# Gate weights through a line in DRAM, and basis groups moved around the batch norms

## The chip, the cores and the metric

The kernel runs on one core of a Trainium2 chip. The metric is device microseconds (us) from start to end of one execution; 510.31 us is the median of 3 runs before the change (509.25 to 510.54).

The core has engines with instruction streams of their own: PE (matrix products; its weight loads are shown apart as PEld), DVE (elementwise work and reductions), ACT (elementwise functions), POOL (here mostly an issuer of transfers) and SP (here only an issuer of transfers). Data lies in SBUF (128 partitions), products come out in PSUM banks of 128 x 512 float32, and transfers between DRAM and SBUF are done by 16 DMA engines.

## The reference, cut to what matters

Four graph layers run over one graph of 512 nodes with 512 features. Each is `x = x + layer(relu(layernorm(x)))`: an attention layer (L0), a GIN of two rounds with batch norm (L1), a GCN (L2) and a gated relational layer of two rounds (L3). The change touches L1's second half, L2 and what L3 needs:

```
# L1, twice (l = 0, 1)
h = x + segment_sum(x[src], dst)
h = prelu(h @ conv_W1[l].T + conv_b1[l], conv_a[l]) @ conv_W2[l].T + conv_b2[l]
x = relu(batchnorm(h) * bn_gamma[l] + bn_beta[l])
# L2
out = leaky_relu(segment_sum((h @ W)[src] * norm, dst) + b)
# L3, twice: weights of each relation r from 30 bases
w[r]  = sum_b att[r, b] * basis[b]                 # basis: 30 x 512 x 512
gate  = sigmoid(x_j @ gate_w[r, :, 0])
msg_r = gate[:, None] * x_j @ w[r]
out   = segment_sum(msg of the edge's type, row) + x @ root + bias
```

## The kernel before

All edges are first counted into dense 512 x 512 matrices, so every segment sum is a product ("gather" below). A 512 x 512 array is held as 4 blocks of 128 partitions, T = 4; P = 128.

**Order of the work.** The source is a trace of instructions in program order. The tool that builds the kernel may let an instruction run earlier or later on its engine when its inputs are planned to be ready; an instruction wrapped in `on(...)` (or `keep_in_program_order`) stays behind the instruction that stands before it in the source on the same engine. An engine carries out its stream in the order so fixed, and waits where an input is late. The products of a gather stand in an `If` of PE alone (`exactly`), which picks one of two arithmetic forms.

**Two streams of bases.** L3's weighted sums over 60 bases of 1 MB are computed while the layers before run. The bases come over SP's queue into 4 buffers (`bases`, AHEAD = 4), in the order of the string `USES`: "P" is a group of 15 (or 7) bases' slices that PE multiplies by a small matrix of attention weights (one `basis_step`, 4 products with 32 output rows each, line 242), "V" is one whole basis that DVE adds into `wrel` in four steps (`advance(more)`, lines 266 to 274, tile `wrel` or `w`). The load of an entry of `USES` is issued when the entry four places before it has been used up, and SP issues in the order of the string. Two PE groups (round l = 0) or three (l = 1) fill one bank `bas`, of which there is only one. After the last of them ACT copies it to SBUF and stores it to DRAM (`leave`, lines 246 to 249); the next group can start only when the copy has read the bank. With `held`, the copy is not put in at once but noted, and put in where `leave()` is called (line 1067).

**The stretch of the change**, in the order of the source:

- Lines 967 to 1022, for l = 0 and 1: the gather into four banks `acc` (for l = 1 at line 976), `advance(more, 3)`, four copies into `aT` by DVE and ACT in turn (lines 978 to 983), then for l = 0 a `basis_step` and four DVE steps, for l = 1 two DVE steps; the first product with a bias and PReLU, two DVE steps after each block; the second product with the batch norm's statistics (`moments`, `normed`). `settle` flips a normalised block (four transposes on PE, line 337) and for l = 0 writes `xn`, which the next gather reads; for l = 1 adds it to `x`. Between the last blocks stand `basis_step(1)` and `basis_step(3 - l)`.
- Lines 1023 to 1027, after l = 1: eight products (two instructions each) for the two gate rows of L3's second round (`gate_rows(1)`: a gate column broadcast along the free axis times the identity, line 809, so that all 128 partitions hold the row), then one `basis_step` whose copy is held.
- Lines 1049 to 1066: L2's layer norm over four blocks, `moments`, `root` (ACT), `scale` (DVE), `normed_to` (ACT), all in `on`; a gather of blocks 0 and 1, then one of blocks 2 and 3. `xn` has two parts: ACT writes the rounded one, DVE the remainder (`F`).
- Lines 1067 to 1079: the held copy, ACT's copies of the gate rows of the second round into the tile `apart`, four copies into `aT`, and products and copies for the gate rows of the first round into two tiles of the pool `rows` (five buffers).
- Lines 1080 to 1091: L2's product, leaky ReLU, layer norm, and after the fourth block `basis_step(3)`, which uses up the last groups. (The `basis_step(1)` at line 1155 then finds none.)
- From line 1149: L3. `Layer.look` (line 1105, DVE) multiplies rows of `h` by a gate row and sums, `begin` (line 1111, PE) multiplies by the root weights, `messages` (line 324) and `end` (line 1145) follow.

Of the forty PE groups, counted from 0, those with number 16 + 3n, 17 + 3n and 18 + 3n belong together in round l = 1. Before the change the group at line 1027 is number 36, the third of its three.

Of the kernel before, what the change touches and what calls it, by code (L numbers as in the profile page):

```python
# [8 lines left out]
F32 = mybir.dt.float32  # L9
# [8 lines left out]
P = 128  # L18
N = 512
D = 512  # L20
T = N // P
# [9 lines left out]
RB = 4  # L31
STEPS = 2
BANKS = 8
USES = "P" * 26 + "VPVVVPPVVVPPPPVVVVPPPPPPPVVVVVVVVVVVV"
FEW = 4095
LESS = 2.0 ** -12
GW = 32
# [12 lines left out]
BQ, BK, B1, CB1, CB2, GAM, BET, GW1, GW2, NCOL = 0, 4, 8, 16, 24, 32, 40, 48, 56, 64  # L50
# [24 lines left out]
def gnn_kernel(ctx: ExitStack, tc: tile.TileContext, out: bass.AP, a: dict):  # L75
    nc = tc.nc
# [4 lines left out]
    rpool = ctx.enter_context(tc.tile_pool(name="rows", bufs=5))  # L81
# [17 lines left out]
    def ps():  # L99
        turn[1] += 1  # L100
        return bank(turn[0][turn[1] % len(turn[0])])
# [20 lines left out]
    ident = const.tile([P, P], F32, name="ident")  # L122
# [22 lines left out]
    cols = const.tile([P, NCOL], F32, name="cols")  # L145
# [8 lines left out]
    apart = const.tile([P, T, N], BF16, name="apart")  # L154
# [64 lines left out]
    dram = ctx.enter_context(tc.tile_pool(name="dram", bufs=1, space=bass.MemoryType.DRAM))  # L219
# [5 lines left out]
    def basis_step(n=1, keep=lambda ins: ins, held=None):  # L225
        for _ in range(n):
            if len(done) == len(loads):
                return
            l, n, g = loads[len(done)]
            done.append(n)  # L230
            assert USES[bases.at] == "P"
            t = bases.take()
            if g == 0:
                sums[:] = [pbas.tile([P, 512], F32, tag="bas", name="bas")]
            if g < STEPS:
                k, at = FULL * NQ, 32 - 2 * NQ * (g + 1)
                lhsT = wide[l][:k, at:at + 32]
            else:
                k = STEPS * HALF_OF * NQ
                lhsT = wide2[:k, :]  # L240
            for j in range(RB):
                tc.keep_in_program_order(nc.tensor.matmul(  # L242
                    sums[0][32 * j:32 * j + 32, :], lhsT=lhsT,
                    rhs=t[:k, j, :], start=(g == 0), stop=(g == STEPS + l - 1)))
            if g == STEPS + l - 1:
                def leave(n=n, bank=sums[0]):
                    o = spool.tile([P, 512], F32, tag="sums", name="sums")
                    keep(nc.scalar.copy(o, bank))  # L248
                    nc.scalar.dma_start(summed[l][n], o)

                if held is None:
                    leave()
                else:
                    held.append(leave)
# [9 lines left out]
    def accumulate(l, to):  # L264

        for b in range(ONPE[l], NB):
            assert USES[bases.at] == "V"
            t = bases.take()
            for r in range(2):
                at = AT1 + 2 * NB * l + NB * r + b  # L270
                for i in range(0, T, 2):
                    on(nc.vector.scalar_tensor_tensor(to[r][:, i:i + 2, :], t[:, i:i + 2, :], scal[:, at:at + 1],  # L272
                                                      to[r][:, i:i + 2, :], op0=ALU.mult, op1=ALU.add))
                    yield
# [51 lines left out]
    def ts(i):  # L326
        return slice(i * P, (i + 1) * P)

    def on(ins):

        return tc.keep_in_program_order(ins)
# [14 lines left out]
    def moments(mv, v, keep=lambda ins: ins):  # L346
        st = stat("st", 6)
        keep(nc.vector.bn_stats(st, v))
        keep(nc.vector.bn_aggr(mv, st))  # L349
# [42 lines left out]
    p = ps()  # L392
# [297 lines left out]
    def advance(gen, n=1):  # L690
        for _ in range(n):
            next(gen, None)
# [15 lines left out]
    plan, passes, at, halves = {}, 0, FIRST, 0  # L708
    waits = None
    for i, what in enumerate(line):  # L710
        at = max(at, FIRST + (len(order) - 2 - FIRST) * passes // whole)
        at = next((e for e in ends if abs(at - e) < 7), at)
# [87 lines left out]
    Cl = late.tile([P, T, N], F32, name="Cl")  # L800
    wrel = [wrel_load(0, r, late.tile([P, T, 512], F32, tag="wrel", name="wrel", bufs=2)) for r in range(2)]
    more = accumulate(0, wrel)
    def gate_rows(l, out):

        banks = [ps() for _ in range(2)]
        for r, p in enumerate(banks):
            for k in range(T):
                at = (GW1, GW2)[l] + 2 * k + r
                on(nc.tensor.matmul(p[:, ts(k)], lhsT=cols[:, at:at + 1].to_broadcast([P, P]), rhs=ident,
                                    start=True, stop=True))  # L810
        yield
        for r, p in enumerate(banks):
            on(nc.scalar.copy(out[r], p))
        yield out

# [149 lines left out]
    for l in range(2):  # L967

        aT = big("E")
        if l:  # L970
            acc = [bank("acc") for _ in range(T)]

            def emit(f, c):
                for m in range(T):
                    product(acc[m], [(f(xn[i][:, k, ts(m)]), Clx[c][:, k, :]) for k in range(T) for i in range(2)])
            exactly(emit)
            advance(more, 3)
        for m in range(T):
            p = acc[m]
            if m % 2:  # L980
                on(nc.vector.tensor_copy(aT[:, m, :], p))  # L981
            else:
                on(nc.scalar.copy(aT[:, m, :], p))
        if l == 0:
            basis_step(1, on)
            advance(more, 4)
        else:
            advance(more, 2)
        w = weights.take()
        h1T = big("B")  # L990
        for m in range(T):
            p = ps()
            product(p, [(w[:, k, ts(m)], aT[:, k, :]) for k in range(T)])
            at = CB1 + T * l + m
            z = small.tile([P, 512], F32, name="z")
            nc.scalar.activation(z, p, AF.Identity, bias=cols[:, at:at + 1])
            u = small.tile([P, 512], F32, name="u")
            nc.vector.tensor_scalar(u, z, 0.0, scal[:, CA + l:CA + l + 1], op0=ALU.min, op1=ALU.mult)
            nc.vector.scalar_tensor_tensor(h1T[:, m, :], z, 0.0, u, op0=ALU.max, op1=ALU.add)
            advance(more, 2)  # L1000
        w = weights.take()
        h2T = big("D")
        if l == 0:
            xn = parts("A", "G")
        for m in range(T):
            p = ps()
            product(p, [(w[:, k, ts(m)], h1T[:, k, :]) for k in range(T)])
            at = CB2 + T * l + m
            on(nc.scalar.activation(h2T[:, m, :], p, AF.Identity, bias=cols[:, at:at + 1]))
            if m:  # L1010
                normed(l, h2T, m - 1, moment)
            moment = stat("mv", 2)
            moments(moment, h2T[:, m, :])
            if m > 1:
                settle(l, h2T, m - 2, xn)
            if l and m < 3:
                advance(more)
        basis_step(1)
        normed(l, h2T, 3, moment)
        settle(l, h2T, 2, xn)  # L1020
        basis_step(3 - l)
        settle(l, h2T, 3, xn)
        if l:
            held = []
            gates = gate_rows(1, [apart.bitcast(F32).rearrange("p t n -> p (t n)")[:, N * r:N * r + N] for r in range(2)])
            next(gates)
            basis_step(1, on, held)

# [7 lines left out]
    def root(t):  # L1038
        on(nc.scalar.activation(sd4[:, t:t + 1], mv[:, t, 1:2], AF.Sqrt, bias=eps))
# [6 lines left out]
    def normed_to(to, t):  # L1046
        on(nc.scalar.activation(to[:, t, :], x[:, t, :], AF.Relu, bias=nm[:, t:t + 1], scale=by[:, t:t + 1]))

    for t in range(T):
        moments(mv[:, t, :], x[:, t, :], on)  # L1050
        root(t)
        if t:
            scale(t - 1)
        if t > 1:
            normed_to(xn[0], t - 2)
    scale(3)
    for t in (0, 1):
        normed_to(h, t)
# [7 lines left out]
    gather((2, 3), apart=True)  # L1066
    for leave in held:
        leave()
    second_w = next(gates)
    aT = big("E")  # L1070
    for m in range(T):
        if m % 2:
# [1 line left out]
        else:  # L1074
            on(nc.scalar.copy(aT[:, m, :], acc[m]))
    l2_b, bias2, bias = rows.take(), rows.take(), rows.take()
    gates = gate_rows(0, [rpool.tile([P, 512], F32, tag="row", name="row") for _ in range(2)])
    next(gates)
    first_w = next(gates)
    h = big("D")  # L1080
    for t in range(T):
        p = ps()
        product(p, [(aT[:, k, ts(t)], w[:, k, :]) for k in range(T)])
        z = small.tile([P, 512], F32, name="z")
        nc.vector.scalar_tensor_tensor(z, p, dinv[:, t:t + 1], l2_b, op0=ALU.mult, op1=ALU.add)
        u = small.tile([P, 512], F32, name="u")
        nc.vector.scalar_tensor_tensor(u, z, SLOPE, z, op0=ALU.mult, op1=ALU.max)
        nc.vector.tensor_add(x[:, t, :], x[:, t, :], u)
        norm_relu(h[:, t, :], x[:, t, :])
        if t == 3:  # L1090
            basis_step(3)

    class Layer:

# [144 lines left out]
```

## Time and profile before

| What | us |
|---|---|
| Median of 3 runs | 510.31 |
| The profiled execution's own time | 511.07 |
| Its span, first to last instruction | 509.1 |
| PE busy | 483.9 (95% of the span) |
| DVE busy | 399.3 (78%) |
| ACT busy | 195.6 (38%) |
| POOL busy | 37.9 (7%) |
| Gate products, line 809, 32 of 275 ns each | in four groups of 8, at 356.45 to 358.4 and 370.52 to 372.46 |
| ACT copies of gate rows, line 813 | 4 of 0.59 |
| One PE group, line 242 | 1.04 to 1.07 |
| One DVE step of a whole basis, line 272 | 1.25 to 1.28 |

How to read it: times inside the execution count from the start of the span. A line of the timeline gives start, duration, engine, line, operation, output and inputs, how many, and in brackets the idle time before it with what ended that. A line of the chain of waits gives start, duration and work of the chain that ended last. A line of the windows gives a stretch, its length, then busy us (and instructions) of PE, PEld, DVE, ACT and POOL, then the TensorE clock that was granted (1 is full), the DMA engines' busy share and GB/s.

### The profile page before, as it was taken

What the parts mean: (1) busy time and instruction counts of PE and PEld (TensorE: products, weight loads), DVE (VectorE), ACT (ScalarE), POOL (GpSimd) and SP (SyncE); (2) the same over time, 40 slices, a digit from 0 to 9 for tenths busy, and PEclk for the clock granted to TensorE, in tenths of its full rate; (3) what the DMA queues carried; (4) which work ended last, traced back from release to release, by engine and by line L of the source; (5) the groups of instructions that cost most, each with busy time, mean ns of one, the idle gap of its engine ahead of it and who ended that gap; (6) DMA issues with size and microseconds to landing.
All of it is one profiled execution on the core that took longest, in us unless ns stands there. A gap on an engine that the chain in (4) does not pass through costs nothing.

```text
span 509.1 us, 5732 instructions
## 1 busy us (share of the span) xinstructions
PE 483.9 (95%) x2014; PEld 249.0 (49%) x2014; DVE 399.3 (78%) x748; ACT 195.6 (38%) x318; POOL 37.9 (7%) x81
## 2 busy tenths in 40 slices
PE   3999999999999999999999999899899999999996
PEld 2333333255564547864445444444654584446642
DVE  6847487879999779999885974797659999998611
ACT  4876779724444213223332134115624610133000
POOL 7000000100000021310040000000010100000000
PEclk9999999999999999999999999999899999999999
DMA  8999768998968499586552695866944965420011
GB/s 243 282 248 250 180 175 194 230 258 198 216 160 198 105 226 293 220 227 191 210 182 84 149 238 195 305 184 156 269 143 154 287 190 217 165 82 3 0 42 41
DMA packets 42951, 94.06 MB, mean 185 GB/s; under 512 B 2113, under 2 KB 2567, under 8 KB 42919
## 3 DMA queue, kind: packets, MB, share of 16 engines
q1 hardware_dynamic: 34682, 68.17, 49.7%
q0 software_dynamic: 5712, 21.07, 13.9%
q10 hardware_dynamic: 2525, 4.39, 2.6%
q8 instruction: 20, 0.33, 0.3%
q14 instruction: 12, 0.10, 0.1%
HBM read 88.38 MB, written 5.24 MB: 184 GB/s over the span
## 4 chain that ended last, share of the span: by engine, by line
PE 67%; DVE 18%; ACT 8%; issue 2%; DMA 2%; ACTq 0%; DVEq 0%
PE pr L324 19%; PE acc L1145 11%; PE pg L324 10%; PE acc L1111 5%; PE ps L484 4%; PE acc L947 3%; PE bas L242 3%; DVE sc L648 3%; ACT sc L649 3%; ACT hs L553 3%; DVE sc L666 3%; PE ao L562 2%; DMA basis<-in_basis 2%; DVE half L642 2%; PE ps L497 2%
## 5 line engine op out<-in xcount | busy, mean ns | idle before, releaser
L272 DVE SCALAR_TENSOR_TENSOR wrel<-basis,scal,wrel 128x1024 f32<-128x1024 f32 x60 | 74.0, 1281 | 3.9 <-DMA basis<-in_basis 3.9
L553 ACT ACTIVATE hs<-iot,key 128x512 f16<-128x512 f16 x75 | 48.8, 711 | 5.5 <-PE ao L562 4.7
L549 DVE TENSOR_SCALAR hd<-iot,key 128x32 f16<-128x32 f16 (+1 forms) x132 | 33.3, 293 | 15.4 <-PE ao L562 15.2
L242 PE MATMUL bas<-basis,wide 120*32 120x512 f32 (+1 forms) x320 | 43.5, 600 | 0.7 <-ACT sums L248 0.7
L272 DVE SCALAR_TENSOR_TENSOR w<-basis,scal,w 128x1024 f32<-128x1024 f32 x32 | 39.3, 1276 | 0.0
L562 PE MATMUL ao<-hs,hd 128*32 128x512 f16 x204 | 25.8, 397 | 2.8 <-ACT hs L553 2.6
L649 ACT ACTIVATE sc<-sc 128x2048 f32<-128x2048 f32 (+1 forms) x10 | 15.7, 1568 | 32.6 <-DVE sc L648 32.6
L484 PE MATMUL ps<-bigB,w 128*128 128x512 f32 x56 | 27.2, 615 | 0.9 <-ACT bigD L487 0.6
L324 PE MATMUL pr<-bigE,w 128*128 128x512 f32 x48 | 21.6, 596 | 1.4 <-DVE bigE L981 1.4
L1195 DVE TENSOR_TENSOR u<-acc,x 128x512 f32<-128x512 f32 (+1 forms) x5 | 2.8, 582 | 23.5 <-PE acc L1145 23.5
L324 PE MATMUL pr<-bigD,w 128*128 128x256 f32 x88 | 20.2, 380 | 0.0
L555 DVE TENSOR_SCALAR hs<-iot,key 128x512 f16<-128x512 f16 x57 | 19.2, 345 | 0.0
L648 DVE TENSOR_TENSOR sc<-sc,half 128x2048 f32<-128x2048 f32 (+1 forms) x10 | 18.6, 1862 | 0.2
L666 DVE TENSOR_TENSOR sc<-sc,rec 128x2048 f32<-128x2048 f32 x8 | 18.3, 2284 | 0.0
L633 PE MATMUL psc<-bigC,bigD 64*128 64x256 f32 x128 | 18.2, 402 | 0.0
L324 PEld LDWEIGHTS pr<-bigD,w 128*128 128x128 f32 x88 | 16.6, 190 | 3.0 <-ACT bigE L891 0.8
L356 ACT ACTIVATE sd<-mv,eps 128x1 f32<-128x1 f32 x16 | 4.7, 296 | 34.4 <-DVE mv L349 33.4
L562 PEld LDWEIGHTS <-hd 128*32 128x32 f16 x204 | 6.1, 94 | 24.2 <-issue 15.4
L324 PE MATMUL pr<-w,bigE 128*128 128x512 f32 x40 | 17.8, 592 | 0.0
L484 PEld LDWEIGHTS ps<-bigB,w 128*128 128x128 f32 x56 | 9.7, 189 | 14.9 <-issue 11.1
L664 DVE RECIPROCAL rec<-ps 128x256 f32<-128x256 f32 x8 | 14.0, 1752 | 3.7 <-PE ps L660 3.7
L635 ACT COPY sc<-psc 128x1024 f32<-128x1024 f32 x16 | 15.6, 1006 | 2.6 <-issue 1.6
(318 smaller groups left out, 960.5 us busy)
## 6 DMA issues: line engine op xcount, KB each, us to landing
basis<-in_basis SPq DMA_DIRECT2D x32, 960.0 KB
basis<-in_basis SPq DMA_DIRECT2D x23, 1024.0 KB
basis<-in_basis SPq DMA_DIRECT2D x16, 448.0 KB
summed<-sums ACTq DMA_DIRECT2D x16, 256.0 KB
w<-in_W POOLq DMA_DIRECT2D x4, 1024.0 KB, 5.6
row<-in_rows POOLq DMA_DIRECT2D x12, 256.0 KB, 7.6
wrel<-summed POOLq DMA_DIRECT2D x4, 512.0 KB, 7.5
w<-in_conv_W1T POOLq DMA_DIRECT2D x2, 1024.0 KB, 5.5
```

Source lines behind the costliest of these rows:

```text
L242: tc.keep_in_program_order(nc.tensor.matmul(sums[0][32 * j:32 * j + 32, :], lhsT=lhsT, rhs=t[:k, j, :], start=(g == 0), stop=(g == STEPS + ...
L272: on(nc.vector.scalar_tensor_tensor(to[r][:, i:i + 2, :], t[:, i:i + 2, :], scal[:, at:at + 1], to[r][:, i:i + 2, :], op0=ALU.mult, op1=AL ...
L324: nc.tensor.matmul(p, lhsT=lhsT, rhs=rhs, start=(i == 0), stop=(i == len(pairs) - 1))
L484: on(nc.tensor.matmul(p, lhsT=w[:, k, ts(m)], rhs=made["hT"][:, k, :], start=(k == 0), stop=(k == T - 1)))
L549: keep(nc.vector.tensor_scalar(hd[:, :w], iot[:, GW * groups_of[c][0]:GW * groups_of[c][0] + w], key[:, 0, c:c + 1], key[:, 2, c:c + 1], o ...
L553: keep(nc.scalar.activation(hs, iot, AF.Sign, bias=key[:, 3, c:c + 1]))
L562: keep(nc.tensor.matmul(cnt[b][GW * (g % T):GW * (g % T) + GW, :], lhsT=hd[:, at:at + GW], rhs=hs, start=(c == in_bank[g][b][0]), stop=(c ...
L648: on(nc.vector.tensor_sub(s, s, half[:, 0:1, :].to_broadcast([P, H // pieces, NH])))
L649: on(nc.scalar.activation(s, s, AF.Exp, scale=HD ** -0.5))
L666: on(nc.vector.tensor_mul(self.sc, self.sc, rec[:, None, :].to_broadcast([P, H, NH])))
L1111: nc.tensor.matmul(self.out[t], lhsT=self.hT[:, k, ts(t)], rhs=self.root[:, k, :], start=(k == 0), stop=False)
L1145: nc.tensor.matmul(self.out[t], lhsT=self.uT[r][:, k, ts(t)], rhs=wrel[r][:, k, :], start=False, stop=(r == 1 and k == T - 1))
```

## The change

`gate_rows` no longer multiplies by the identity. Four transfers on POOL's queue write the gate columns (128 partitions x 4 values each) as rows into a small DRAM tile `lines`, element by element; four more read a row and spread it to 128 partitions, two into `apart`, right after those of the first four in the source, and two into tiles of `rows`, at the old place. One PE group moves from the batch norm of l = 0 (3 groups there become 2) to the place after the gather of l = 1, and one DVE step there moves ahead of the `aT` copies (3 + 2 becomes 4 + 1); one group moves from the end of L2 (3 become 2) to the held place at line 1027 (1 becomes 2). `USES` changes to match: in "PPPPVVVV" the fourth P and the first V change places. In L2's norm, `normed_to` of block t - 2 is put ahead of `root(t)` and `scale(t - 1)`.

```diff
@@ -31,7 +31,7 @@
 RB = 4
 STEPS = 2
 BANKS = 8
-USES = "P" * 26 + "VPVVVPPVVVPPPPVVVVPPPPPPPVVVVVVVVVVVV"
+USES = "P" * 26 + "VPVVVPPVVVPPPVPVVVPPPPPPPVVVVVVVVVVVV"
 FEW = 4095
 LESS = 2.0 ** -12
 GW = 32
@@ -800,18 +800,19 @@
     Cl = late.tile([P, T, N], F32, name="Cl")
     wrel = [wrel_load(0, r, late.tile([P, T, 512], F32, tag="wrel", name="wrel", bufs=2)) for r in range(2)]
     more = accumulate(0, wrel)
+
+    lines = dram.tile([2, 2, 512], F32, name="lines")
+    for l, at in enumerate((GW1, GW2)):
+        for r in range(2):
+            nc.gpsimd.dma_start(lines[l, r].rearrange("(k p) -> k p", p=P),
+                                a["cols"][:, at + r:at + 2 * T:2].rearrange("p k -> k p"))
+
     def gate_rows(l, out):
-
-        banks = [ps() for _ in range(2)]
-        for r, p in enumerate(banks):
-            for k in range(T):
-                at = (GW1, GW2)[l] + 2 * k + r
-                on(nc.tensor.matmul(p[:, ts(k)], lhsT=cols[:, at:at + 1].to_broadcast([P, P]), rhs=ident,
-                                    start=True, stop=True))
-        yield
-        for r, p in enumerate(banks):
-            on(nc.scalar.copy(out[r], p))
-        yield out
+        for r in range(2):
+            nc.gpsimd.dma_start(out[r], lines[l, r:r + 1, :].to_broadcast([P, 512]))
+        return out
+
+    second_w = gate_rows(1, [apart.bitcast(F32).rearrange("p t n -> p (t n)")[:, N * r:N * r + N] for r in range(2)])
 
 
 
@@ -974,7 +975,7 @@
                 for m in range(T):
                     product(acc[m], [(f(xn[i][:, k, ts(m)]), Clx[c][:, k, :]) for k in range(T) for i in range(2)])
             exactly(emit)
-            advance(more, 3)
+            advance(more, 4)
         for m in range(T):
             p = acc[m]
             if m % 2:
@@ -985,7 +986,8 @@
             basis_step(1, on)
             advance(more, 4)
         else:
-            advance(more, 2)
+            basis_step(1, on)
+            advance(more)
         w = weights.take()
         h1T = big("B")
         for m in range(T):
@@ -1018,13 +1020,11 @@
         basis_step(1)
         normed(l, h2T, 3, moment)
         settle(l, h2T, 2, xn)
-        basis_step(3 - l)
+        basis_step(2)
         settle(l, h2T, 3, xn)
         if l:
             held = []
-            gates = gate_rows(1, [apart.bitcast(F32).rearrange("p t n -> p (t n)")[:, N * r:N * r + N] for r in range(2)])
-            next(gates)
-            basis_step(1, on, held)
+            basis_step(2, on, held)
 
 
 
@@ -1048,11 +1048,11 @@
 
     for t in range(T):
         moments(mv[:, t, :], x[:, t, :], on)
+        if t > 1:
+            normed_to(xn[0], t - 2)
         root(t)
         if t:
             scale(t - 1)
-        if t > 1:
-            normed_to(xn[0], t - 2)
     scale(3)
     for t in (0, 1):
         normed_to(h, t)
@@ -1066,7 +1066,6 @@
     gather((2, 3), apart=True)
     for leave in held:
         leave()
-    second_w = next(gates)
     aT = big("E")
     for m in range(T):
         if m % 2:
@@ -1074,9 +1073,7 @@
         else:
             on(nc.scalar.copy(aT[:, m, :], acc[m]))
     l2_b, bias2, bias = rows.take(), rows.take(), rows.take()
-    gates = gate_rows(0, [rpool.tile([P, 512], F32, tag="row", name="row") for _ in range(2)])
-    next(gates)
-    first_w = next(gates)
+    first_w = gate_rows(0, [rpool.tile([P, 512], F32, tag="row", name="row") for _ in range(2)])
     h = big("D")
     for t in range(T):
         p = ps()
@@ -1088,7 +1085,7 @@
         nc.vector.tensor_add(x[:, t, :], x[:, t, :], u)
         norm_relu(h[:, t, :], x[:, t, :])
         if t == 3:
-            basis_step(3)
+            basis_step(2)
 
     class Layer:
 
```

## The prediction

> **What bounds the kernel now.** I read the page's shares first (PE busy 95% of the span), then the chain of waits, which says where PE's lost time lies, then the timelines of PE, DVE and ACT around each edit, then windows of 1 us for the granted clock. The chain from the first batch norm to L2, with the pieces that the change touches:
>
> ```profile
> 308.81 1.04 PE bas L242 x8
> ...
> 309.87 9.96 DMA basis<-in_basis
> ...
> 319.85 2.56 DVE wrel L272 x3
> ...
> 323.44 0.69 DVE bigE L981
> ...
> 361.56 9.11 PE acc L947 x32
> 370.68 0.89 PE pg L809 x8
> 371.57 0.89 PE pr L809 x8
> ...
> 386.20 2.76 PE bas L242 x24
> ```
>
> It is a chain of PE work with one detour: a basis for DVE lands at 319.85, DVE's steps on it stand ahead of the copy of `aT` that the next product reads, and PE waits. The timelines of PE show that wait, and a second one before L2's gather:
>
> ```profile
> 313.95 0.66 PE L337 MATMUL pg<-ident,bigD 128*128 128x128 f32 x4
> ...
> 324.18 6.28 PE L324 MATMUL pr<-bigE,w 128*128 128x512 f32 x14 [1.43 <-DVE bigE L981]
> ...
> 356.45 1.95 PE L809 MATMUL pr<-ident,cols 128*128 128x128 f32 x16
> 358.33 1.06 PE L242 MATMUL bas<-basis,wide 112*32 112x512 f32 x8
> 361.56 3.62 PE L947 MATMUL acc<-R,bigC 128*128 128x512 f32 x8 [2.17 <-ACT bigC L1047]
> ```
>
> The windows show what the second wait does besides: the column after POOL's is the granted clock.
>
> ```profile
> 360.00:361.00 1.00, 0.00 (x0) 0.00 (x0) 0.90 (x6) 0.58 (x2) 0.00 (x0) 1.00 1.05 270
> 361.00:362.00 1.00, 0.44 (x2) 0.37 (x3) 0.90 (x5) 0.69 (x3) 0.00 (x0) 0.86 1.06 254
> 362.00:363.00 1.00, 1.00 (x4) 0.81 (x3) 0.62 (x4) 1.00 (x3) 0.00 (x0) 0.50 1.07 217
> ```
>
> After 2.17 us of idle the clock fell to half until about 365.1 and the gather took 9.11 us, where 32 products at the 0.23 us of its later ones are 7.3: some 1.8 us lost.
>
> **Part 1: the group and the basis that change places (l = 0 to l = 1).** Now four groups lie in the norm of l = 0. The last flip started at 313.95, though ACT had its input ready at 313.25 (the timeline's last L852 starts at 312.44 and takes 0.81). With one group fewer the flip starts at about 313.3 and the gather, which ran without a break from 314.36 to 321.73, is over at 321.1. The V load is issued when the entry four places before it is used up. That becomes the third V, whose last step DVE ended at 298.84, where it was a PE group ending at 309.87; even with the crowded landing of 9.96 us the basis is there by 309. So DVE's four steps (4 x 1.25 = 5.0) run from the last remainder at 315.3 to 320.3, and the copies to `aT` (0.69 each) end at 321.0 and 321.9, before the product comes to them. The moved group takes over the freed load slot at 309.87 (same 9.96 at worst, landing at 319.85) and costs its 1.04 from 321.1 to 322.1, where the product begins. Before, two of its instructions ran early (2 x 0.43) and the rest from 324.18, which is worth a start at 323.3. Gain: **1.2 us**. Bounds: if DVE's wait and PE's 1.43 stay as they are, the group costs 1.04 and saves 0.65, a loss of 0.4; if the group fell into a wait, a gain of 1.9.
>
> **Part 2: `normed_to` ahead of `root`.** PE waited for the first block of `bigC`, which ACT began at 360.62, behind a `root` that waited for a third block's statistics. Its own operand `nm` was written at 359.56. So it can start at 359.6 and the gather at 360.55, 1.0 us sooner. The remainders `F` come 0.5 us sooner (their copies start at 362.1, not 362.63), and PE reaches them 3.4 us after its start as now. I take **0.9**; between 0 and 1.0.
>
> **Part 3: gate products gone, a second held group.** The 16 instructions at 356.45 lay in the wait: nothing is gained, and the hole opens. Group 36 now runs at 356.45 and PE idles from 357.5 to 360.55: 3.05 us where it was 2.17. The 16 at 370.68 are on the chain, 1.78 us. They also hid the copies to `aT` (until 371.55); without cover about 0.2 of these would show.
>
> The second held group, number 37, is the first of a new bank, and there is one bank `bas`. It waits for the held copy of group 36, which stands on ACT behind the four blocks' norms and ended at 367.43. So group 37 can't fill the hole. It is queued on PE behind group 36 alone, and may fall after the gather of blocks 0 and 1 or after both. The trace has such a case: six of the second round's L1111 products, earlier in the source than the `If`s of `messages`, ran at 465.46 after four of them. After both, it costs its 1.06 and hides the `aT` copies: 1.78 - 1.06 = 0.7 gained. Between the two, it waits about 0.9 for the copy and leaves 0.2 of the copies bare: 1.78 - 1.06 - 0.9 - 0.2, a loss of 0.4. I take **0.7**, since the nearest row is the L1111 one.
>
> At the end of L2 two groups are left of three (386.20, 2.76): 0.92 less work, but the flip of the last block at 394.15 followed ACT's normalised block (ended 394.01) at once, and that depends on DVE, busy without gaps from 379. I take **0**; up to 0.9 if root products are put ahead of that flip. DVE's later work moves with L2's first output, and its lead at the first `end` (a step ends at 423.2, PE needs it at 424.8) covers the rest.
>
> **Part 4: the clock.** By the trace, 2.17 us of idle brought half clock, so 3.05 will: **0** against before. A gain of 1.8 if the low stretch misses the gather.
>
> The Trainium skill, "TensorE: Matmul & The Clock Gate", section "Part 1: The HAM clock gate", says that the clock falls to half after at least one idle window of some 3.4 us, and that the window runs free of the kernel. By that rule neither hole is long enough to be sure of it, and the time would be about 1.8 lower than by the row; the row decides.
>
> **Part 5: transfers.** Four element-wise writes of 512 elements and four row spreads of 256 KB. POOL has no work from 13.4 to 39.16, so the writes can be issued there: 0.55 to 0.76 each by the other issues, 3 us in all, and nothing queued behind them is due before Wo at 39.16. Their duration is not in the trace. The nearest row is `cols` (128 pieces of 256 bytes, 3.8 us to landing): below, 3.8 for one; above, four times as many pieces, four transfers, one after the other: 61 us, ending by 75. The spread into `apart` must wait for its last reader (L627, 153.6) and is read at 433.3; the spreads into `rows` find their buffers free after 275 and are read at 387.25; row loads took 3.8 to 11.8 us. So waits of these readers cost **0**. What the small pieces take from others: the DMA engines are over 90% busy until 50 us, but a basis group runs at 31.02, 39.69, 48.23 and 54.43 on loads issued from 4.43 to 18.6, with four buffers ahead. Bounds: 0, and 7 us if for all of 61 us the loads ran at half speed (30.5 behind) with a lead of only the 23.4 from the first to the fourth of these groups. I take **0**, since four loads lie ahead. ACT loses four copies of 0.59 off the path.
>
> The Trainium skill, "DMA: Bandwidth & Descriptors", section "Rules for kernel authors", says that a strided last dimension becomes one descriptor per element and advises to rearrange. That speaks against this edit: 2048 pieces of 4 bytes. No row here shows one.
>
> **Sum.** -1.2 - 0.9 - 0.7 + 0 = -2.8 us. The profiled execution, 511.07 (span 509.1 and 1.97 around it), becomes 508.3; the median, 0.76 lower, 510.31 - 2.8 = **507.5**. The edits' own range: 505.8 (part 1 at 1.9, part 2 at 1.0, the end of L2 at 0.9) to 508.6 (group 37 between the gathers).
>
> **Rivals.**
>
> *The held copy stops PE (slower).* If group 37 keeps its place ahead of the gather, PE waits until the copy of group 36 ends: 367.43, less the 0.9 by which ACT is sooner, 366.5; group until 367.6; gather at 9.11 cold until 376.7; `aT` copies 0.2; less part 1's 1.2: a product start of 375.7 against 372.46. That is +3.2: **513.5**. It decides once the gather starts more than 2.8 us later than now, at 364.4 on the old clock (372.46 + 1.2 - 9.3). For it: group 37 precedes both gathers in the source. Against: the L1111 row, where PE went on to an `If`.
>
> *The gain stays in part 1's wait (no change).* V's place changes, but DVE still waits or the moved group does (loads crowd 316 to 325 at up to 410 GB/s), so part 1 costs 0.4: -0.9 - 0.7 + 0.4 = -1.2: **509.1**. For it: 9.96 us landings; against: the V load is issued 11 us sooner.
>
> *Clock and end as well (faster still).* The low stretch misses the gather (-1.8) and the flip's place lets 0.9 through: **504.8**. Small chance, two things together.
>
> *The small pieces delay the early loads (slower).* Up to +7 against -2.8: **514.5**; DMA engines full to 50 us speak for it, the lead of four buffers against it. That the rows don't arrive as said is excluded: their readers would wait at 387 and 433.
>
> **Numbers.** Forecast 0.47, faster still 0.09, no change 0.21, held copy 0.19, early loads 0.04. A measurement here tells about 0.3% (1.53 us): faster below 508.78, slower above 511.84. Faster 0.56, same 0.21, slower 0.23. The range takes in the forecast's, most of the stronger gain and the no-change cases, and ends at 512.2, short of the held copy's centre: 505.2 to 512.2.
>
> **What would show it.** Right: no DVE wait on a basis near 320, `aT` product starting about 322; first `bigC` about 359.6; idle near 3 us before the gather with the clock at 0.5 after it; no L809; group 37 as eight `bas` instructions behind a gather; two groups after L2's product. Wrong: `bas` ahead of the gather behind ACT's copy (L248), a wait at 321 on a basis, PE waits on basis loads before 60 us, a full clock at 361.

## The result and the profile after

| | median us | runs | ratio to before |
|---|---|---|---|
| before | 510.33 | 4 (509.25 to 510.54) | |
| after | 524.05 | 4 (520.57 to 524.92) | 1.0268 [1.0222, 1.0315] |

The changed kernel is 2.7% slower, 13.7 us, where 2.8 us less was forecast. The profiled execution took 523.93 (span 521.8), 12.9 more than the one of before (511.07). One of the six executions of the run e1 below took 524.66, over 1.5% more than the fastest of them, and is left out as slow (the median would be 518.87 with it); every other time is of fast executions. Following the same piece of work through both timelines gives where it went:

| Start of | before | after | later by |
|---|---|---|---|
| PE group on the second early basis | 39.69 | 49.52 | 9.8 |
| PE group on the fifth early basis | 62.65 | 74.15 | 11.5 |
| PE group ahead of l = 1 | 308.74 | 320.27 | 11.5 |
| second product of l = 1 | 337.16 | 347.58 | 10.4 |
| last flip of its norm | 355.96 | 369.80 | 13.8 |
| L2's product | 372.30 | 386.00 | 13.7 |
| first root product of L3 | 390.23 | 403.74 | 13.5 |
| end of the span | 509.1 | 521.8 | 12.7 |

So 11.5 are lost before 75 us, 1.1 are won at the group that changed places, and 3.4 are lost in the batch norm of l = 1. The chain of waits of the changed kernel shows the first loss: it puts 44 us down to a load of a basis.

```profile
5.01 44.46 DMA basis<-in_basis
49.48 0.04 issue
49.52 1.24 PE bas L242 x8
```

PE's timeline of before at that place, where no group waits for its basis:

```profile
31.02 1.24 PE L242 MATMUL bas<-basis,wide 120*32 120x512 f32 x8
...
39.69 1.22 PE L242 MATMUL bas<-basis,wide 120*32 120x512 f32 x8
40.55 0.39 PE L562 MATMUL ao<-hs,hd 128*32 128x512 f16 x3
40.87 1.98 PE L484 MATMUL ps<-bigB,w 128*128 128x512 f32 x4
```

The changed kernel:

```profile
35.67 1.94 PE L242 MATMUL bas<-basis,wide 120*32 120x512 f32 x8 [4.81 <-DMA basis<-in_basis]
37.38 0.65 PE L562 MATMUL ao<-hs,hd 128*32 128x512 f16 x3
37.96 3.00 PE L484 MATMUL ps<-bigB,w 128*128 128x512 f32 x4
...
49.52 1.24 PE L242 MATMUL bas<-basis,wide 120*32 120x512 f32 x8 [2.89 <-DMA basis<-in_basis]
50.51 0.66 PE L562 MATMUL ao<-hs,hd 128*32 128x512 f16 x3
51.10 3.26 PE L484 MATMUL ps<-bigB,w 128*128 128x512 f32 x4
```

Two waits, 7.70 us together, and after each the products run slowly: four of L484 take 3.00 and 3.26 where 1.98 is usual before. Windows of 4 us of the changed kernel (granted clock, DMA share and GB/s are the last three columns):

```profile
17.00:21.00 4.00, 4.00 (x12) 1.58 (x10) 3.90 (x27) 3.07 (x6) 0.60 (x1) 1.00 1.23 172
21.00:25.00 4.00, 4.00 (x17) 1.22 (x18) 3.27 (x16) 3.41 (x6) 0.00 (x0) 1.00 2.15 38
25.00:29.00 4.00, 3.69 (x18) 1.29 (x18) 2.98 (x13) 3.36 (x7) 0.00 (x0) 1.00 0.44 32
29.00:33.00 4.00, 1.86 (x10) 0.36 (x8) 1.00 (x5) 2.40 (x4) 0.00 (x0) 1.00 0.98 114
33.00:37.00 4.00, 1.33 (x8) 0.39 (x11) 0.00 (x0) 0.00 (x0) 0.00 (x0) 0.53 1.65 114
```

The same windows of the kernel before:

```profile
21.00:25.00 4.00, 4.00 (x18) 1.47 (x14) 3.43 (x18) 3.19 (x6) 0.00 (x0) 1.00 1.05 234
25.00:29.00 4.00, 3.69 (x18) 1.04 (x17) 2.56 (x12) 3.37 (x7) 0.00 (x0) 1.00 1.03 233
```

From 21 to 29 us some 35 GB/s arrive in place of 233, with a busy share of the DMA engines of 2.15 and 0.44. In these microseconds the four small writes are under way: issued from 13.2 to 17.6, they land a median of 23.1 us after their issue, the slowest 32.8. Across the wait of 4.81 the clock then falls to half (0.53).

The stretch of l = 1 in the timeline of the changed kernel, which answers to the waits at 324.18 and 361.56 shown of before:

```profile
332.75 1.07 PE L242 MATMUL bas<-basis,wide 120*32 120x512 f32 x8
333.75 1.98 PE L324 MATMUL pr<-bigE,w 128*128 128x512 f32 x4
335.57 1.02 PE L324 MATMUL pg<-bigE,w 128*128 128x512 f32 x2
336.42 5.31 PE L324 MATMUL pr<-bigE,w 128*128 128x512 f32 x12
...
366.35 0.66 PE L337 MATMUL pr<-ident,bigD 128*128 128x128 f32 x4 [2.72 <-ACT bigD L853]
366.94 2.93 PE L242 MATMUL bas<-basis,wide 120*32 120x512 f32 x16
...
373.29 1.07 PE L242 MATMUL bas<-basis,wide 112*32 112x512 f32 x8 [2.37 <-DMA basis<-in_basis]
374.86 3.51 PE L948 MATMUL acc<-R,bigC 128*128 128x512 f32 x8 [0.51 <-ACT bigC L1047]
378.21 2.00 PE L948 MATMUL acc<-R,F 128*128 128x512 f32 x8
381.08 1.07 PE L242 MATMUL bas<-basis,wide 120*32 120x512 f32 x8 [0.87 <-ACT sums L248]
```

The moved group stands ahead of the product and no wait for a basis is left there. But the product is now cut up: half of the first block (`pr` x4), a quarter of another (`pg` x2), then the rest. In the norm behind it PE waits 2.72, and two groups take 2.93 where two took 1.92 before. The second held group stands between the two gathers and waits 0.87 for the copy (L248).

### The profile page after: what moved, and what is told of

It reads as the page before. It is cut to its first block, busy times and chain, and to the rows that moved or that the text cites. A ratio compares the mean times of both kernels' runs of the same rounds, so it can differ in the third digit from the quotient of the medians.

```text
span 521.8 us, 5673 instructions
## 1 busy us (share of the span) xinstructions
PE 486.7 (93%) x1982; PEld 246.0 (47%) x1982; DVE 399.2 (77%) x748; ACT 193.1 (37%) x314; POOL 44.3 (8%) x89
## 4 chain that ended last, share of the span: by engine, by line
PE 54%; DVE 26%; DMA 9%; ACT 8%; issue 2%; SPq 1%; ACTq 0%; DVEq 0%
PE pr L324 12%; PE acc L1142 11%; DMA basis<-in_basis 9%; PE pg L324 7%; DVE wrel L272 6%; PE acc L1108 5%; PE bas L242 3%; DVE sc L648 3%; PE ps L484 3%; ACT sc L649 3%; DVE sc L666 3%; PE acc L948 2%; DVE st L348 2%; ACT hs L553 2%; DVE half L642 2%
## 5 line engine op out<-in xcount | busy, mean ns | idle before, releaser
L242 PE MATMUL bas<-basis,wide 120*32 120x512 f32 (+1 forms) x320 | 45.6, 628 | 11.6 <-DMA basis<-in_basis 10.1
L484 PE MATMUL ps<-bigB,w 128*128 128x512 f32 x56 | 29.5, 659 | 0.9 <-ACT bigD L487 0.6
L242 PEld LDWEIGHTS bas<-basis,wide 120*32 120x32 f32 (+1 forms) x320 | 8.3, 110 | 25.8 <-issue 18.1
L484 PEld LDWEIGHTS ps<-bigB,w 128*128 128x128 f32 x56 | 10.6, 208 | 17.0 <-issue 13.2
L324 PE MATMUL pr<-w,bigE 128*128 128x512 f32 x40 | 17.9, 595 | 0.0
```

The costliest lines, as they stand in the source:

```text
L242: tc.keep_in_program_order(nc.tensor.matmul(sums[0][32 * j:32 * j + 32, :], lhsT=lhsT, rhs=t[:k, j, :], start=(g == 0), stop=(g == STEPS + ...
L324: nc.tensor.matmul(p, lhsT=lhsT, rhs=rhs, start=(i == 0), stop=(i == len(pairs) - 1))
L484: on(nc.tensor.matmul(p, lhsT=w[:, k, ts(m)], rhs=made["hT"][:, k, :], start=(k == 0), stop=(k == T - 1)))
```

## The experiments

Times of before, taken beside each set of runs, were 509.64, 509.55, 509.63 and 509.56. "Straight" means that the two layers' rows, laid one after the other, are an input `gw` of the kernel and are spread from there. "By the ratios" below means the difference of two ratios of the table, times 509.6.

| Run | median us | against before | ratio |
|---|---|---|---|
| e1: rows by lines, nothing moved | 516.69 | +7.05 | 1.0149 [1.0104, 1.0193] |
| e2: moves only | 514.33 | +4.69 | 1.0094 [1.0077, 1.0111] |
| e3: after, rows straight | 512.67 | +3.03 | 1.0057 [1.0039, 1.0075] |
| e4: before, rows straight | 508.25 | -1.39 | 0.9966 [0.9952, 0.9981] |
| f1: `normed_to` first | 508.35 | -1.20 | 0.9969 [0.9956, 0.9983] |
| f2: group and basis change places | 513.49 | +3.94 | 1.0063 [1.0039, 1.0087] |
| f3: f2, product's order held | 510.15 | +0.60 | 1.0010 [0.9996, 1.0025] |
| f4: second held group | 511.12 | +1.57 | 1.0025 [1.0011, 1.0039] |
| g1: e1, writes late | 512.95 | +3.32 | 1.0070 [1.0054, 1.0086] |
| g2: e1, writes of whole rows | 507.62 | -2.01 | 0.9965 [0.9954, 0.9977] |
| g3: e1, half of the pieces | 509.87 | +0.24 | 1.0027 [1.0003, 1.0052] |
| g4: e4 with f1 | 507.32 | -2.31 | 0.9951 [0.9933, 0.9968] |
| i1: f1, first layer's rows straight | 507.01 | -2.55 | 0.9943 [0.9924, 0.9962] |
| i2: g4, group behind both gathers | 507.62 | -1.94 | 0.9957 [0.9941, 0.9973] |
| i3: e1, writes behind the casts | 508.85 | -0.71 | 0.9984 [0.9964, 1.0004] |

### The rows apart from the moves: e1 to e4

e1 is before with the changed `gate_rows`:

```diff
+    lines = dram.tile([2, 2, 512], F32, name="lines")
+            nc.gpsimd.dma_start(lines[l, r].rearrange("(k p) -> k p", p=P),
+                                a["cols"][:, at + r:at + 2 * T:2].rearrange("p k -> k p"))
...
+            nc.gpsimd.dma_start(out[r], lines[l, r:r + 1, :].to_broadcast([P, 512]))
```

> The kernel before with the gate rows by the line in DRAM (the four small writes and the four row loads as in the changed kernel), and nothing moved. Theory A (the small pieces starve the early basis loads; the moves matter little): the first product on Wo is late by the 11.5 us seen between the two traces (62.57 against 74.07 for W1), basis loads crawl between 21 and 37 us; the 16 gate products off the path give back up to 1.8: 519.5 to 522. Theory B (the small pieces' delay is taken up later, the moves of groups and norms cost the time): 508.5 to 511, with no late basis that lasts past 75 us.

e2 is the changed kernel with the products with `ident` back in `gate_rows` and at their old places.

> The changed kernel with the gate products by the identity put back where they stood, so all the moves of groups, loads and norms, and no transfer for the rows. Theory A: part 1 gains some 1.1 before the product of l = 1, the norm of l = 1 loses some 3.4 in the trace of the changed kernel, the rest is nearly level: 511 to 514. Theory B: 520 to 524. What I forecast for the moves alone (-1.2 and -0.9, held group between the gathers at 0 to +0.9): 508 to 509.

e3 is the changed kernel, and e4 is e1, both without the four writes and with

```diff
-            nc.gpsimd.dma_start(out[r], lines[l, r:r + 1, :].to_broadcast([P, 512]))
+            nc.gpsimd.dma_start(out[r], a["gw"][2 * l + r:2 * l + r + 1, :].to_broadcast([P, 512]))
```

> The changed kernel, with the rows loaded from an input in which the four rows lie one after the other: no small writes, all the rest as in the changed kernel. Theory A: the 11.5 us before 75 us are gone, what the moves cost stays: 510.5 to 513. Theory B: 520 to 524, the time of the changed kernel. If the loss in the norm of l = 1 comes only from loads that the small pieces made late: 507 to 508.5, my forecast.

> The kernel before, with the rows loaded from an input in which they lie one after the other, no gate products and nothing moved. The 16 products at 370.68 (1.78 us) leave the path, the copies to aT come bare by 0.2, and the 16 at 356.45 only open the hole: 508.5 to 509. If the wider hole costs more clock: 510 to 511. Theory A puts it at 508.5 to 509.5, 11 us under the first of these runs; theory B level with the first.

e1 and e4 differ in the four writes and in where the spreads read; that is 516.69 - 508.25 = 8.4 us by the medians, 9.3 by the ratios. With the moves in place the same difference is 524.05 - 512.67 = 11.4 (the changed kernel against e3). The moves cost 4.7 with the products in place (e2) and 512.67 - 508.25 = 4.4 without (e3 against e4); the products' absence alone wins 1.4. So of the 13.7 of the change the writes are 8 to 11 and the moves 4 to 5: theory A, with moves dearer than it had them. The timeline of e1:

```profile
37.82 1.93 PE L242 MATMUL bas<-basis,wide 120*32 120x512 f32 x8 [7.51 <-DMA basis<-in_basis]
...
51.40 1.06 PE L242 MATMUL bas<-basis,wide 120*32 120x512 f32 x8 [2.54 <-DMA basis<-in_basis]
```

Waits of 10.05, and what the low clock adds to the products behind them (1.93 for 1.24, and four of L484 in 3.08 and 3.66 for 1.98: 3.5), make 13.5; the group at 62.65 of before starts there at 76.05, 13.4 later. This profiled execution took 521.04 and is one of the slower ones: the times of e1 spread from 514.96 to 521.84, those of e2, which has no writes, from 514.27 to 514.42. How long the writes hold the loads varies from execution to execution, and so the size of this loss is known only as 8 to 11.

### The moves one by one: f1 to f4

f1:

```diff
         moments(mv[:, t, :], x[:, t, :], on)
+        if t > 1:
+            normed_to(xn[0], t - 2)
         root(t)
         if t:
             scale(t - 1)
-        if t > 1:
-            normed_to(xn[0], t - 2)
```

> The kernel before with only the order of normed_to and root changed. My forecast of this step: 0.9 less, 508.5 to 509 where before is 509.6. Rival: the shorter wait of PE is given back, since PE then waits for the next block or for the copies F: 509.3 to 510.

The 1.2 is the forecast, if anything a little more. The timeline shows PE's wait down from 2.17 to 1.17, and the windows a clock that stays full through the gather, of which the first microsecond is shown:

```profile
358.03 1.15 PE L947 MATMUL acc<-R,bigC 128*128 128x512 f32 x4 [1.17 <-ACT bigC L1047]
359.33 1.16 PE L947 MATMUL acc<-R,bigC 128*128 128x512 f32 x4 [0.16 <-ACT bigC L1047]
360.98 2.11 PE L947 MATMUL acc<-R,F 128*128 128x512 f32 x8 [0.48 <-DVE F L1059]
```

```profile
358.00:359.00 1.00, 0.97 (x4) 0.67 (x4) 0.93 (x4) 0.81 (x2) 0.00 (x0) 1.00 1.05 248
```

From the last flip of the norm to L2's product it takes 14.91 us here (353.42 to 368.33) and took 16.34 before (355.96 to 372.30). Of these 1.4, 1.0 is the sooner start of the gather. The full clock adds only 0.4, since PE, now faster, waits 0.16 for the second block and 0.48 for the remainder `F`.

f2 takes `USES`, the `advance` counts, the `basis_step` ahead of l = 1 and the `basis_step(2)` from the change:

```diff
-            advance(more, 2)
+            basis_step(1, on)
+            advance(more)
...
-        basis_step(3 - l)
+        basis_step(2)
```

> The kernel before with only the group and the basis that change places. Theory A (the order of the products of l = 1 costs more than the group gains): the first product starts about 1.1 sooner, the first block's flip in the norm comes 1.7 later, and the total is 1.5 to 3 more: 511 to 512.7. Rival B (the held group alone costs): 508.3 to 509.

f3 adds to it

```diff
-            product(p, [(w[:, k, ts(m)], aT[:, k, :]) for k in range(T)])
+            for k in range(T):
+                on(nc.tensor.matmul(p, lhsT=w[:, k, ts(m)], rhs=aT[:, k, :], start=(k == 0), stop=(k == T - 1)))
```

> The same with the first product of conv held in the order of the source, block by block, as the kernel before ran it. Theory A: the loss goes and the 1.1 of part 1 stays, 508 to 509. If the late norm comes from something else than the order (DVE's steps on the basis that ran in the wait before): 511 to 512.7 as the run without the pinned order.

Holding the product's order takes 513.49 - 510.15 = 3.3 us out of f2 (2.7 by the ratios). The line is in the loop, so it holds the product of l = 0 too; but that one starts at 280.19 in f3 and at 280.20 before, in the same order, so the 3.3 belong to l = 1. What the order does is seen in DVE's first step on that product (`u<-z`). Before, with the product starting at 321.73 and going on at 324.18; then f2, started at 322.61; then f3, started at 322.15:

```profile
328.64 0.48 DVE L998 TENSOR_SCALAR u<-z,scal 128x512 f32<-128x512 f32 x1 [1.53 <-ACT z L996]
```

```profile
330.50 0.48 DVE L999 TENSOR_SCALAR u<-z,scal 128x512 f32<-128x512 f32 x1 [5.22 <-ACT z L997]
```

```profile
326.61 0.48 DVE L1000 TENSOR_SCALAR u<-z,scal 128x512 f32<-128x512 f32 x1 [1.70 <-ACT z L998]
```

Cut up, the product finishes its first block at about the time of its second, so DVE idles 5.22 and then has all blocks' work before it, with its steps on bases between: the norm's first statistics start at 344.31 in f2, at 342.71 before and at 340.69 in f3. PE does the same work in the same time (13.83 us from the first product to the second in f2, 13.84 in f3), but the end of the stretch hangs on the first block.

f3 is still not the 1.2 faster that was forecast. In the two profiled executions the gain is there: the second product starts at 335.99 in f3 and at 337.16 before. But the wait of 1.43 that the swap was to remove is not in every execution. Of twelve profiled executions with the old place of the group, five show it (1.43 to 1.68), two show 0.18 and 0.28, five show none; of the last, g4, in DVE's timeline:

```profile
318.06 3.68 DVE L272 SCALAR_TENSOR_TENSOR wrel<-basis,scal,wrel 128x1024 f32<-128x1024 f32 x3 [2.50 <-DMA basis<-in_basis]
```

The basis is there at 318.06, not at 319.85, and PE begins the product at 321.32 and goes through it without a wait. From the second group of l = 0's norm to the second product it takes 26.84 us before, with the wait, 25.68 in f3 and 25.44 in g4, without it: the swap wins 1.2 against an execution with the wait and loses 0.2 against one without. Over many executions that would be a gain below the forecast, but not the 0.6 lost by the medians (f3's interval reaches down to a gain of 0.2); where the rest lies stays open.

f4:

```diff
-            basis_step(1, on, held)
+            basis_step(2, on, held)
...
-            basis_step(3)
+            basis_step(2)
```

> The kernel before with only the second held group (two groups in the norm of l = 1, two in L2 in place of one and three). By the trace of the moves alone, the group stands between the two gathers, waits about 1.1 for the copy and takes 1.0, against 0.9 saved in L2: 1.2 to 1.7 more, 510.8 to 511.4. By my upper bound, a group between the gathers: 0.4 to 0.9 more. Rival: it costs nothing here, and the swap carries all 4.7: 509.3 to 510.

Its timeline has the second group between the gathers:

```profile
365.12 2.26 PE L947 MATMUL acc<-R,F 128*128 128x512 f32 x8
367.79 1.06 PE L242 MATMUL bas<-basis,wide 120*32 120x512 f32 x8 [0.40 <-ACT sums L248]
368.78 2.12 PE L947 MATMUL acc<-R,bigC 128*128 128x512 f32 x8
```

That is 0.4 + 1.0 on the path, and of the 0.9 saved in L2 only 0.3 reaches the first root product (17.6 us after L2's product starts, 17.9 before): 1.6 more by the times. The moves alone add to -1.2 + 3.9 + 1.6 = 4.3, against 4.7 together (e2). By the ratios it is 2.9 against 4.8, so the parts may not make up the whole; one thing that differs is the wait for the copy, 0.40 in f4 and 1.16 in e2.

### The writes: number, form and time: g1 to g3, i3

g2 copies whole rows at the same place on the same queue; g3 leaves two of the four writes in pieces and takes the other rows straight:

```diff
-            nc.gpsimd.dma_start(lines[l, r].rearrange("(k p) -> k p", p=P),
-                                a["cols"][:, at + r:at + 2 * T:2].rearrange("p k -> k p"))
+            nc.gpsimd.dma_start(lines[l, r:r + 1, :], a["gw"][2 * l + r:2 * l + r + 1, :])
```

> As the first run, at the same place and on the same queue, but each of the four writes copies a row of 2 KB that lies in one piece. If it is the pieces of 4 bytes that cost: 508 to 509.5. If it is four more transfers ahead of the early loads, or the way through DRAM: 517 to 522 as the first run.

```diff
-        for r in range(2):
+        for r in range(1):
             nc.gpsimd.dma_start(lines[l, r].rearrange("(k p) -> k p", p=P),
```

> As the first run, but only two of the four writes are made in pieces, early; the other two rows come straight from the input. If the delay goes by the number of pieces: about half of 10 over the rows loaded straight, 512 to 515. If the lead of the basis loads takes up half of them: 508 to 510. If one transfer of this kind already stops the loads: 517 to 520.

With whole rows the loss is gone, 507.62 against 516.69 (windows of g2; 257 GB/s where the changed kernel has 38):

```profile
21.00:25.00 4.00, 4.00 (x17) 1.29 (x18) 3.52 (x19) 3.41 (x6) 0.00 (x0) 1.00 1.03 257
```

So it is the form of the writes, not four more transfers, nor the way through DRAM. Half of the pieces cost 509.87 - 508.25 = 1.6 by the medians and 3.1 by the ratios, where all cost 8.4 and 9.3. In the trace of g3 the first basis is waited for 1.32 us, no second one, and the clock stays full: there the lead takes up most of what half of the pieces do. Other executions of g3 took up to 514.36, so that the cost is less than in proportion is likely and not sure.

g1 and i3 make the same writes late. g1 ties them to a small transfer from DVE; i3 pins them behind POOL's casts:

```diff
+    blank = stat("blank")
+    on(nc.vector.memset(blank, 0.0))
+    nc.gpsimd.dma_start(lines.rearrange("l r n -> (l r) n")[:, 0:1], blank[0:4, :])
```

> As the first run (rows by the line in DRAM, nothing moved), but the four writes wait for a small transfer after the count of edges, some 235 us into the kernel, where the DMA engines are busy 40 to 60%. If the small writes cost only where the loads have no lead (my theory): 508.3 to 510.5, the time of the rows loaded straight. If they hold back the loads of bases for 20 us wherever they run: 513 to 520.

```diff
-    Clx = rounded(Cl, "R0")
+    Clx = rounded(Cl, "R0", on)
...
+            on(nc.gpsimd.dma_start(lines[l, r].rearrange("(k p) -> k p", p=P),
+                                a["cols"][:, at + r:at + 2 * T:2].rearrange("p k -> k p")))
```

> As the first run, with the four writes issued some 259 us into the kernel, behind the casts on POOL, and nothing else shifted. If the writes cost only where the basis loads have no lead: 508 to 509.5. If they hold back the basis loads there too: a PE or DVE wait on a basis after 265 us, and 511 to 515. Where their slowness reaches the loads of rows or weights instead, those waits show it.

g1 misled: 4.7 over e4, but only 0.17 of it is a wait of PE itself for a basis. (Another 1.68 lies behind DVE's steps on a late basis at the place of the 1.43 above, a wait that executions without the writes show as well.) Behind its extra transfer POOL's casts began at 257.06 (255.66 in e4), they fell on a DVE step (2.85 us for 0.75), PE waited 1.81 for a block behind it, and the clock fell to 0.71. i3 has the writes without that. A window of it, and from its timeline the one wait of PE that may go back to a basis, one of the two short ones counted above:

```profile
264.00:268.00 4.00, 4.00 (x14) 2.31 (x13) 2.24 (x4) 0.62 (x1) 0.36 (x1) 1.00 1.57 10
```

```profile
323.04 6.28 PE L324 MATMUL pr<-bigE,w 128*128 128x512 f32 x14 [0.28 <-DVE bigE L980]
```

Here too the busy share is high (1.57) at few GB/s (10), and PE does not notice: in e4 the DMA engines move nothing at all from 264 to 272, so there was little to hold back. i3 lies 0.6 over e4, and the intervals overlap.

### Both gains, the hole and the other place: g4, i1, i2

g4 is e4 with f1's edit.

> The rows loaded straight (508.25 against 509.64 alone) with normed_to ahead of root (508.35 against 509.55 alone), nothing else moved: 506.6 to 507.5 if both gains add; 508 to 508.5 if both come out of the same wait before the gather.

Most of both gains add (1.4 and 1.2 alone, 2.3 together). i1 is f1 with only the first layer's rows taken straight, so that the second layer's sixteen products stay in the idle stretch:

```diff
-    gates = gate_rows(0, [rpool.tile([P, 512], F32, tag="row", name="row") for _ in range(2)])
-    next(gates)
-    first_w = next(gates)
+    first_w = [rpool.tile([P, 512], F32, tag="row", name="row") for _ in range(2)]
+    for r in range(2):
+        nc.gpsimd.dma_start(first_w[r], a["gw"][r:r + 1, :].to_broadcast([P, 512]))
```

> normed_to ahead of root, the rows of the first layer loaded straight from an input with whole rows, and the second layer's sixteen products with the identity left in the idle stretch ahead of the gather. In the run with only normed_to moved PE idled 1.17 there and the clock stayed at 1.00; with all rows loaded it idled 2.44 and the gather ran at 0.50. If the clock takes the difference: 508.35 less the 1.78 of the products at 370.68, 506.4 to 506.8, under the 507.3 of all rows loaded straight. If the products only fill time that is free anyway: 507.1 to 507.6.

Timelines of g4, then i1, at the gather:

```profile
358.78 3.75 PE L941 MATMUL acc<-R,bigC 128*128 128x512 f32 x8 [2.44 <-ACT bigC L1039]
```

```profile
361.13 2.46 PE L947 MATMUL acc<-R,bigC 128*128 128x512 f32 x8 [1.17 <-ACT bigC L1047]
```

From there to L2's product it takes 10.20 in g4 (368.98) and 8.71 in i1 (369.84), so in these two executions the filled hole keeps the clock full and saves 1.5 us. The medians differ by 0.3, less than their intervals: what the clock is worth over many executions stays open.

i2 places the second group of the norm behind the held copy:

```diff
     for leave in held:
         leave()
+    basis_step(1)
...
-            basis_step(3)
+            basis_step(2)
```

> The rows loaded straight with normed_to ahead of root (507.3), and the second group of the norm placed after both gathers, where my forecast had it. My forecast of this place: 1.06 for the group against 0.92 less in L2, so 507.2 to 507.7. If the group disturbs what follows L2 as it did between the gathers (1.6 more): 508.5 to 509.

0.3 over g4, within both intervals: in the place that the forecast gave it, the group costs no more than was forecast, as far as these runs can tell. i1 (507.01) and g4 (507.32) are faster than both kernels of the change.

## Why the prediction was wrong

- **Part 5, transfers: the step that failed.** "I take **0**, since four loads lie ahead": e1 against e4 gives 8.4 (9.3 by the ratios), and the changed kernel against e3 11.4. The lead was counted in buffers, but the loads that fill these buffers were still on the way while the writes ran: issued from 4.43 to 21.66 in the changed kernel, they kept PE waiting at 35.67 and 49.52. The bound was mis-sized too: it let the loads run at half speed, and 38 of 234 GB/s is a sixth; and the waits carry the low clock behind them (3.5 of 13.5 in the trace of e1), which the bound left out. The rival of the early loads had the mechanism, its place (PE waits on basis loads before 60 us) and its sign, and was given 0.04. The rest of the part holds: the spreads are waited for by nobody, and POOL's queue held nothing urgent. A write's issue took 1.1, not 0.55 to 0.76.
- **Part 1: two steps failed.** The group and DVE's steps were priced, the order of the product behind them was not: it changes with what stands ahead of it, and that is 3.3 us (f2 against f3). And the gain was taken from a wait that one execution had, and that five of twelve show. With the order held, the steps of the part came as written (f3's product starts at 322.15, forecast 322.1; the second product 1.2 sooner), yet the median of f3 is 0.6 slower, inside the stated bounds (a gain of 1.9 to a loss of 0.4) only by its interval. In the changed kernel itself the 1.1 did arrive at the product, as said, before the norm gave back 3.4.
- **Part 2: right.** 0.9 forecast, 1.2 measured (ratio 0.9956 to 0.9983). The gather starts 1.0 sooner, as said; that the shorter hole also keeps the clock full, and that PE then waits for `F`, was not foreseen.
- **Part 3.** Removing the products: 1.4 by e4; 1.78 was on the chain, but from the last flip to L2's product only 0.8 of it shows in the trace of e4 (15.54 for 16.34), whose gather has the low clock for longer behind a wider hole (3.58). The held group fell between the gathers, not behind both: the step "I take **0.7**, since the nearest row is the L1111 one" failed. The row was also misread: the six L1111 products at 465.46 ran after three products in an `If`, not four, and the fourth came behind them, so the row itself showed work falling in between. The bound for this place, a wait of 0.9, has 0.87 in the trace of the changed kernel (0.40 to 1.16 in the others). The price of 1.06 for the place behind both agrees with i2. At L2's end 0 was taken and 0.3 came.
- **Part 4: right.** The clock was low in the gather as the row said (the one at 374.86 begins with 3.51 for eight products), though the hole came in two pieces, 2.37 in wait for a basis and, behind one group, 0.51. By the windows the clock fell to half after holes of 1.76 (f2), 2.17 (before), 2.44 (g4) and 3.58 (e4), and not after one of 1.17 (f1). The Trainium skill, "TensorE: Matmul & The Clock Gate", section "Part 1: The HAM clock gate", asks for an idle window of some 3.4 us; the holes of 1.76 to 2.44 are shorter and brought it nevertheless, so the row was the better guide.
- **The rival of the held copy** did not happen as priced: PE went through the first gather before it met the group.
- The Trainium skill, "DMA: Bandwidth & Descriptors", section "Rules for kernel authors", advises against a strided last dimension because it becomes one descriptor per element. g2 against e1 agrees with the advice, 9.1 us apart by the medians; the descriptors themselves stand in no view here. The forecast named the rule and gave it no time.

## What to carry to other kernels

Do not price a transfer of a few kilobytes by its bytes when it goes in 4-byte pieces. Here four of 2 KB cost 8 to 11 us beside loads that PE needed, and 0.6 or nothing where the DMA engines would have idled (i3); laid so that they go in rows, they cost nothing that shows (g2). The lead of four buffers did not cover this, as the loads into them had not landed yet. When work is put ahead of a product, look at the order in which the product's blocks will then come out: what waits behind it starts with the first block. And a wait read from one execution is a gain only as often as other executions have it.

## What the runs showed that was not expected

- 2048 pieces of 4 bytes show in the page of e1 as only 192 packets and 0.03 MB more than in e4, yet they held the moved bytes at 28 to 38 GB/s for 8 us and PE waited 10 us for two early bases. Whether it is the reading of single elements or the writing of them was not tried.
- SP's queue was slower beside POOL's writes: the issue of `Wv`, 2.11 us before, took 11.06 in the changed kernel and 17.14 in e1. From the timelines of SP, before and changed:

```profile
18.67 2.11 SPq L160 DMA_DIRECT2D w<-in_Wv  x1
```

```profile
21.71 11.06 SPq L160 DMA_DIRECT2D w<-in_Wv  x1
```

- A DVE step (`bigA<-bigA,rstd,row`) that began with POOL's four casts took 2.85 us in g1, ending 0.6 after they did; its three sisters took 0.75. In e4, with the casts begun earlier, three DVE steps took 0.89 to 0.98 and the casts 3.27 for 2.28.
